# Two-layer graph-and-sequence kernel: set-up loads in another order, single buffers in other memory, offsets of four instruction streams

## The chip, the cores and the metric

The kernel runs on one core of one Trainium2 chip. A core has four compute engines: TensorE (PE, with its weight loads shown as PEld), VectorE (DVE), ScalarE (ACT) and GpSimd (POOL); SyncE (SP) issues most of the DMAs here. Each engine executes its own instructions in order and waits on semaphores for the others. The metric is the device time of one execution in microseconds (us), the median of several runs.

## The reference, cut to what matters

Input x is 32 batch elements of 512 nodes with 256 features; adj is a 512 x 512 matrix of 0 and 1 for each element. Two layers, each a graph attention and a sequence block, both on a layer norm of x and added to it:

```python
x = x + L0_gnn(layernorm(x), adj, ...)   # 4 heads, masked softmax over neighbours, norm per head
x = x + L0_ffn(layernorm(x), ...)        # Mamba-2 block: W_in, conv of 4, chunked scan, norm, W_out, W_lin
x = x + L1_gnn(layernorm(x), adj, ...)   # 1 head, masked softmax, elu
x = x + L1_ffn(layernorm(x), ...)        # LSTM over the 512 steps, all 32 elements at once,
                                         # argmax gate, prefix and suffix sums
```

The first three lines are independent for each batch element. The last one walks through the 512 steps for all elements together, so it starts only when every element is through the first three.

## The kernel before, in words

`layers_per_batch` does the first three lines, `recurrence` the last. A second copy of `layers_per_batch` for general adjacency values stands behind a branch and is not executed with these inputs.

`layers_per_batch` begins with a set-up. `load_k` (line 96) and `load_row` (line 101) load the weights on SP's queue, one DMA each; `load_row` sends one row of HBM to all 128 partitions. Weights that only the set-up needs (w0t, asrc, adst, normw, woutt, wlin, w1t, a1) lie in the pool `wset`. From them PE and DVE make derived weights: the score weights sw0 (from `pwa`, lines 154 and 205) and sw1 (from `pwb`, lines 166 and 212), and wc, the product of W_out and W_lin (`pwc`, lines 243 and 247). Then `setup.close()` gives the memory of `wset` back, and the pools `io`, `one` and `two` are opened over it.

The work on an element is cut into generators that yield after each small step: `plain0` (graph attention of layer 0, lines 470 to 580), `after0` (its norm per head, lines 315 to 338), `mamba_in` and `mamba_dt` (layer norm, transposes and the time-step column of the Mamba block), `mamba` (the block itself), and `plain1` (graph attention of layer 1). `plain0` begins with two loads, adj (line 474) and x (line 476); then come the layer norm (lines 65 to 71), `x+beta` on POOL (line 479), the mask `msk` and the check `sqa` from adj, transposes into xT, `exponents` (pra, mall, mxa, rowsa, linea, pca), the transposed mask adjT from `pm`, the projection `phn` with its copies hn and hb, and the weighted sums (rb, w, pav, psu, psut, pavT). `mamba` ends with ssc, its reciprocal root (`rstd_of`, tiles ve and rs on POOL, lines 54 and 56) and the update of x (line 848).

Four streams of such parts are merged: each part has a start and an end in units of one element's period, relative to `mamba` of the same element (0 to 1), and the step with the smallest due time is emitted next. `PACE` places the steps within `mamba`.

```python
    streams = [
        each((0.0, 1.0, mamba, 0)),
        each((-0.097, -0.026, mamba_in, 0), (-0.026, 0.192, mamba_dt, 0)),
        each((0.571, 0.86, second, -1), (0.86, 1.54, first, 2)),
        each((1.65, 1.76, after0, 2)),
    ]
```

A fifth stream is `recurrence_weights` (lines 1030 to 1108): it scales and reorders the LSTM's weights on POOL and writes them to an HBM buffer `wr`, through small tiles with one buffer each. Its due times start at 3.25. The framework's scheduler then reorders what was emitted on each engine by its own estimate of when operands are ready, so an instruction with no operand from the elements can come far ahead of its due time; in the trace these weights are prepared between 18 and 142 us.

All loads and stores of elements go through SP's queue: adj, x, the spread rows rb and bc, ce, and the store X of each element after layer 1 (line 862). One buffer holds adj, four hold x.

## Time and profile before

| what | us |
|---|---|
| median of 3 runs | 4829.85 |
| lowest and highest | 4828.24, 4832.57 |
| the profiled execution's own time | 4838.21 |
| its span, first to last instruction | 4836.4 |
| busy: PE, PEld | 4191.4, 2651.5 |
| busy: DVE, ACT, POOL | 3279.3, 3068.7, 1308.8 |
| adj of elements 0, 1, 2, 3 issued at | 30.0, 37.6, 80.3, 178.4 |
| first zs of mamba, elements 0, 1, 2 | 130.7, 230.2, 330.6 |
| X stored, elements 0, 29, 30, 31 (issue) | 317.9, 3249.9, 3324.5, 3369.3 |
| mean granted TensorE clock | 0.965 |

Busy is the time in which an engine executes an instruction. The page cuts the span into 40 slices of 121 us and shows busy tenths for each. The timeline lists instructions with start, duration, and in brackets the idle time of the engine just before them and what ended it. "SPq" and "ACTq" are DMA issues by those engines' sequencers. A load is asked for at its issue and can be used some microseconds later; the trace shows both ends, the issue by SPq and the first instruction that had waited for it. Durations below come from the profiled execution, which took 8.4 us more than the median.

### The profile page before, as it was taken

The numbers are of one execution on the slowest core, as the hardware profiler recorded it, in microseconds if no ns is written. First come the engines' busy times: TensorE is split into PE (matmuls) and PEld (weight loads), VectorE is DVE, ScalarE is ACT, GpSimd is POOL, SyncE is SP. The second block draws the span as 40 slices with busy tenths as digits, with TensorE's granted clock in tenths as the row PEclk, the third lists the DMA queues.
The fourth block names the chain that finished last, engine by engine and source line by source line (L and its number), as shares of the span: only waits on it lengthen the run. The fifth ranks groups of instructions, "written<-read, shape, count | busy, mean of one in ns | idle before, by whom it ended". The sixth has DMA issues, their size and how long they took to land. (4 is left out here: it accounts for less than half of the span.)

```text
span 4836.4 us, 126769 instructions
## 1 busy us (share of the span) xinstructions
PE 4191.4 (87%) x52926; PEld 2651.5 (55%) x52926; DVE 3279.3 (68%) x8670; ACT 3068.7 (63%) x6724; POOL 1308.8 (27%) x1012
## 2 busy tenths in 40 slices
PE   4888888888888888888888888886999999999993
PEld 2444444444554444544445444544777777777772
DVE  3567666676666666666666666664677777777776
ACT  2677667776677767677677776764555555555552
POOL 4333343333433334333343333431000000000000
PEclk7899999999999999999999999998999999999997
DMA  3221122211222112221112211111111111111115
GB/s 109 64 67 61 55 70 66 65 62 55 67 65 69 57 60 62 71 69 57 60 59 73 69 57 60 53 44 60 37 39 42 38 43 41 41 40 39 42 39 159
DMA packets 273746, 288.34 MB, mean 60 GB/s; under 512 B 152844, under 2 KB 224488, under 8 KB 270984
## 3 DMA queue, kind: packets, MB, share of 16 engines
q1 hardware_dynamic: 269784, 270.26, 19.0%
q10 hardware_dynamic: 3216, 9.81, 0.7%
q8 instruction: 418, 6.85, 0.6%
q14 instruction: 168, 1.38, 0.1%
q0 software_dynamic: 160, 0.04, 0.0%
HBM read 226.04 MB, written 37.11 MB: 54 GB/s over the span
## 5 line engine op out<-in xcount | busy, mean ns | idle before, releaser
L1260 PEld LDWEIGHTS pg<-wall,h 128*32 128x32 f32 x24528 | 476.7, 109 | 228.5 <-DVE h L1335 226.8
L1260 PE MATMUL pg<-wall,h 128*32 128x64 f32 x24528 | 561.2, 239 | 34.6 <-DVE h L1335 10.6
L1236 PE MATMUL pu<-xTr,wall 128*128 128x256 f32 x2048 | 565.5, 399 | 0.0
L467 DVE SCALAR_TENSOR_TENSOR w<-w,adjT 128x1024 f32<-128x1024 f32 x256 | 348.2, 1381 | 247.4 <-ACT w L461 247.4
L1320 ACT ACTIVATE z<-pg 128x64 f32<-128x64 f32 (+1 forms) x1536 | 345.8, 241 | 129.9 <-PE pg L1260 90.2
L1237 ACT ACTIVATE xu<-pu,wall 128x256 f32<-128x256 f32 x512 | 243.2, 475 | 278.6 <-PE pu L1236 278.6
L743 ACT ACTIVATE g<-bc,cs 128x128 f32<-128x128 f32 x1024 | 322.0, 391 | 139.7 <-PE py L811 139.7
L693 DVE SCALAR_TENSOR_TENSOR acc<-px,convw,acc 128x511 f32<-128x511 f32 (+2 forms) x480 | 347.3, 746 | 76.6 <-ACT acc L688 68.7
L461 ACT ACTIVATE w<-rb,neg,colsa 128x512 f32<-128x512 f32 x512 | 387.5, 806 | 10.2 <-DMA rb<-linea 5.8
L1236 PEld LDWEIGHTS pu<-xTr,wall 128*128 128x128 f32 x2048 | 348.8, 190 | 63.7
L533 PE MATMUL pav<-w,hb 128*64 128x512 f32 x1024 | 352.6, 615 | 21.9 <-DVE w L467 21.9
L830 PE MATMUL po<-wc,xh 128*128 128x256 f32 x1024 | 282.8, 422 | 96.8 <-POOL xh L800 96.8
L729 POOL TENSOR_TENSOR ce<-ce,cT 128x384 f32<-128x384 f32 x128 | 185.1, 1475 | 667.2 <-ACT cT L701 650.3
L54 POOL TENSOR_SCALAR ve<-mv 128x4 f32<-128x4 f32 x32 | 6.2, 193 | 1317.5 <-DVE mv L1161 1317.5
L1250 PE MATMUL pg<-turner,xu 128*32 128x64 f32 (+2 forms) x12288 | 324.3, 238 | 0.4 <-issue 0.3
L945 PE MATMUL pov<-wb,wv 128*128 128x257 f32 x1024 | 246.2, 393 | 90.4 <-DVE wv L467 90.4
L672 PE MATMUL px<-mT,win 128*128 128x512 f32 x640 | 306.9, 610 | 0.0
L830 PEld LDWEIGHTS po<-wc,xh 128*128 128x128 f32 x1024 | 203.1, 212 | 141.4 <-POOL xh L800 111.1
L1330 ACT ACTIVATE tc<-z 128x64 f32<-128x64 f32 x512 | 131.6, 257 | 224.1 <-DVE z L1328 224.1
L945 PEld LDWEIGHTS pov<-wb,wv 128*128 128x128 f32 x1024 | 193.6, 194 | 135.3 <-DVE wv L467 105.6
L1250 PEld LDWEIGHTS pg<-turner,xu 128*32 128x32 f32 x12288 | 265.6, 110 | 3.0 <-issue 1.8
L56 POOL TENSOR_TENSOR rs<-ve,mhalf 128x4 f32<-128x4 f32 (+1 forms) x192 | 256.0, 1334 | 15.9
(245 smaller groups left out, 8615.4 us busy)
## 6 DMA issues: line engine op xcount, KB each, us to landing
bc<-line SPq DMA_DIRECT2D x128, 512.0 KB
adj<-in_adj_dram SPq DMA_DIRECT2D x32, 1024.0 KB
rb<-linea SPq DMA_DIRECT2D x64, 512.0 KB
ce<-line SPq DMA_DIRECT2D x64, 384.0 KB
x<-in_x_dram SPq DMA_DIRECT2D x32, 512.0 KB
X<-x SPq DMA_DIRECT2D x32, 512.0 KB
xt<-X SPq DMA_DIRECT2D x128, 128.0 KB
x<-X SPq DMA_DIRECT2D x128, 128.0 KB
```

What stands on the lines that cost most here:

```text
L461: nc.scalar.activation(w[:, t, k, :], rb[:, k, :], AF.Relu, bias=neg1, scale=cols[:, 2 * m + t, h + k : h + k + 1],)
L467: nc.vector.scalar_tensor_tensor(w[:, :, k, :], w[:, :, k, :], 1.0, edges, ALU.add, ALU.mult)
L533: nc.tensor.matmul(pa[k * HO : (k + 1) * HO, :], hb[:, j, 2 * q + k, :], w[:, t, k, :], start=(j == 0), stop=(j == NT - 1),)
L672: nc.tensor.matmul(pz, win[:, k, col : col + P], mT[:, k, :], start=(k == 0), stop=(k == DK - 1))
L693: nc.vector.scalar_tensor_tensor(acc[:, s:], pz[:, : N - s], convw[:, cc, k : k + 1], acc[:, s:], ALU.mult, ALU.add)
L743: nc.scalar.activation(g[:, i, k, :], bc[:, k, i * P : (i + 1) * P], AF.Relu, bias=cs[:, i, 2 * cc + k : 2 * cc + k + 1], scale=-1.0,)
L830: nc.tensor.matmul(po[:, i * D : (i + 1) * D], xh[:, cc, it * P : (it + 1) * P], wc[:, cc, :], start=(cc == 0), stop=(cc == NC - 1),)
L945: nc.tensor.matmul(po[:, : D + 1], ws[j // 2][:, j % 2, 0, it * P : (it + 1) * P], wb[:, j, :], start=(j == 0), stop=(j == NT - 1),)
L1236: nc.tensor.matmul(pu, wih[:, k, u, :], xT[:, k, :], start=(k == 0), stop=(k == DK - 1))
L1250: nc.tensor.matmul(p[q * GB : (q + 1) * GB, :], xu[:, 2 * q + half, r : r + GB], turner[:, s:e], start=True, stop=(t == 0),)
L1260: nc.tensor.matmul(p[q * GB : (q + 1) * GB, :], h[:, k, :], whh[:, k, q, s:e], start=(start and k == 0), stop=(k == DK - 1),)
L1320: nc.scalar.activation(z[:, J + s0 : J + e0], p[:, : e0 - s0], AF.Tanh)
```

## The change

It has four parts. The loads of the set-up get another order on the same queue: first x of element 0, then w0t, asrc, adst, w0, adj of element 0, then beta and the other rows, then the Mamba weights, and last those for layer 1 and wc. For this the pool `io` is opened before the set-up, so that x and adj of element 0 have memory of their own, and `plain0` uses them for b = 0.

Five tiles of the Mamba part with one buffer each (csr, ce, bT, cT, ssr) move from the pool `one` to a new pool `mam`, opened where `wset` was closed, so they take the set-up's memory.

Each tile of `recurrence_weights` is now begun by a POOL copy of one column of the x of the element that is current in the merge (`begun`, `now`). So the tile's loads cannot start before that x is there.

Some offsets of the streams and of `PACE` change in the second or third digit.

```diff
+    io = ctx.enter_context(tc.tile_pool(name="io", bufs=2))
+    def load_x(b):
+        x = io.tile([P, NT, D], F32, tag="x", bufs=4, name=f"x{b}")
+        nc.sync.dma_start(out=x, in_=a.x[b].rearrange("(i p) d -> p i d", p=P))
+        return x
+    def load_adj(b):
+        adj = io.tile([P, NT, N], I32, tag="adj", bufs=1, name=f"adj{b}")
+        nc.sync.dma_start(out=adj, in_=a.adj[b].rearrange("(i p) j -> p i j", p=P))
+        return adj
+    x0 = load_x(0)
...
-    w0 = load_k(a.w0, D, "w0")
     w0t = load_k(a.w0t, D, "w0t", wset)
     asrc = load_k(a.asrc, T0, "asrc", wset)
     adst = load_k(a.adst, T0, "adst", wset)
+    w0 = load_k(a.w0, D, "w0")
+    adj0 = load_adj(0)
+    beta = load_row(a.beta, "beta")
     bias0 = load_row(a.bias0, "bias0")
     gamma = load_row(a.gamma, "gamma")
-    beta = load_row(a.beta, "beta")
+    alog = load_row(a.alog, "alog")
+    blin = load_row(a.blin, "blin")
     win = load_k(a.win, DIN, "win")
     convw = load_k(a.convw, 4, "convw")
     convb = load_k(a.convb, 1, "convb")
     dtb = wp.tile([NH, 1], F32, name="dtb")
     nc.sync.dma_start(out=dtb, in_=a.dtb.rearrange("o h -> h o"))
-    alog = load_row(a.alog, "alog")
     dcol = load_k(a.dcol, 1, "dcol")
+    w1t = load_k(a.w1t, D, "w1t", wset)
+    a1 = load_k(a.a1, 2, "a1", wset)
+    w1 = load_k(a.w1, D, "w1")
     normw = load_k(a.normw, 1, "normw", wset)
     woutt = load_k(a.woutt, DI, "woutt", wset)
     wlin = load_k(a.wlin, D, "wlin", wset)
-    blin = load_row(a.blin, "blin")
-    w1 = load_k(a.w1, D, "w1")
-    w1t = load_k(a.w1t, D, "w1t", wset)
-    a1 = load_k(a.a1, 2, "a1", wset)
...
     setup.close()
-    io = ctx.enter_context(tc.tile_pool(name="io", bufs=2))
+    mam = ctx.enter_context(tc.tile_pool(name="mam", bufs=1))
...
+        x, adj = (load_x(b), load_adj(b)) if b else (x0, adj0)
...
-        csr = one.tile([P, N], F32, tag="csr", name=f"csr{b}")
+        csr = mam.tile([P, N], F32, tag="csr", name=f"csr{b}")
...
-    PACE = ((0, 0.0), (10, 0.4), (17, 0.693), (STEPS[mamba], 1.0))
+    PACE = ((0, 0.0), (10, 0.41), (17, 0.7), (STEPS[mamba], 1.0))
...
-        each((-0.097, -0.026, mamba_in, 0), (-0.026, 0.192, mamba_dt, 0)),
-        each((0.571, 0.86, second, -1), (0.86, 1.54, first, 2)),
-        each((1.65, 1.76, after0, 2)),
+        each((-0.117, -0.026, mamba_in, 0), (-0.004, 0.184, mamba_dt, 0)),
+        each((0.571, 0.86, second, -1), (0.86, 1.52, first, 2)),
+        each((1.65, 1.75, after0, 2)),
...
+        now = lambda: states[int(min(at))]["x"][:, 0, 0:1]
-        streams.append(3.25 + (nb - 8) / 64 * n for n, _ in enumerate(recurrence_weights(nc, rw, a, wr)))
+        streams.append(3.25 + (nb - 8) / 64 * n for n, _ in enumerate(recurrence_weights(nc, rw, a, wr, now)))
...
+    def begun(t, *columns):
+        for n in columns or (0,):
+            nc.gpsimd.tensor_copy(t[:, n : n + 1], now())
+        return t
...
-                raw = tile_(P, 4 * J, f"rwraw{q % 2}")
+                raw = begun(tile_(P, 4 * J, f"rwraw{q % 2}"))
```

The same goes for ce, bT, cT and ssr as for csr, and for the tiles rwl, rbl, the two small rwraw and the rwt of fw and bw as for the last line.

More of the change, by code (lines that the diff above doesn't have):

```diff
@@ L340, in attention0 @@
     def attention0(b, state):
-        adj = io.tile([P, NT, N], I32, tag="adj", bufs=1, name=f"adj{b}")
-        nc.sync.dma_start(out=adj, in_=a.adj[b].rearrange("(i p) j -> p i j", p=P))
-        x = io.tile([P, NT, D], F32, tag="x", bufs=4, name=f"x{b}")
-        nc.sync.dma_start(out=x, in_=a.x[b].rearrange("(i p) d -> p i d", p=P))
+        x, adj = (load_x(b), load_adj(b)) if b else (x0, adj0)
         xn = two.tile([P, NT, D], F32, tag="rowa", name=f"xn{b}")
@@ L470, in plain0 @@
     def plain0(b, state):
-        adj = io.tile([P, NT, N], I32, tag="adj", bufs=1, name=f"adj{b}")
-        nc.sync.dma_start(out=adj, in_=a.adj[b].rearrange("(i p) j -> p i j", p=P))
-        x = io.tile([P, NT, D], F32, tag="x", bufs=4, name=f"x{b}")
-        nc.sync.dma_start(out=x, in_=a.x[b].rearrange("(i p) d -> p i d", p=P))
+        x, adj = (load_x(b), load_adj(b)) if b else (x0, adj0)
         xn = two.tile([P, NT, D], F32, tag="rowa", name=f"xn{b}")
@@ L654, in mamba_dt @@
         yield
-        ce = one.tile([P, NC, N - P], F32, tag="ce", name=f"ce{b}")
+        ce = mam.tile([P, NC, N - P], F32, tag="ce", name=f"ce{b}")
         for k in range(2):
@@ L682, in mamba @@
         xh = two.tile([P, NC, N], F32, tag="wide", bufs=4 if odd is not None else 3, name=f"xh{b}")
-        bT = one.tile([DS, N], F32, tag="bT", name=f"bT{b}")
-        cT = one.tile([P, N], F32, tag="cT", name=f"cT{b}")
+        bT = mam.tile([DS, N], F32, tag="bT", name=f"bT{b}")
+        cT = mam.tile([P, N], F32, tag="cT", name=f"cT{b}")
         def convolved(cc):
@@ L837, in mamba @@
             nc.tensor.matmul(pss[32 * cc : 32 * (cc + 1), :], ones[:, :32], zs[:, cc, :], start=True, stop=True)
-        ssr = one.tile([P, N], F32, tag="ssr", name=f"ssr{b}")
+        ssr = mam.tile([P, N], F32, tag="ssr", name=f"ssr{b}")
         nc.scalar.copy(ssr, pss)
@@ L1027, in layers_per_batch, with recurrence_weights @@
         nc.vector.tensor_scalar(odd, pf[:1, :1], P - 0.5, None, ALU.is_lt)
-def recurrence_weights(nc, pool, a, wr):
+def recurrence_weights(nc, pool, a, wr, now):
     Q, J = 4, 64
@@ L1052, in ordered @@
         return t
-    wl = tile_(P, 2 * DK, "rwl")
+    def begun(t, *columns):
+        for n in columns or (0,):
+            nc.gpsimd.tensor_copy(t[:, n : n + 1], now())
+        return t
+    yield
+    wl = begun(tile_(P, 2 * DK, "rwl"), 0, DK)
     for q in range(Q):
@@ L1063, in recurrence_weights @@
     nc.gpsimd.tensor_tensor(wl[:, :DK], wl[:, DK:], wl[:, :DK], ALU.subtract)
-    bl = tile_(P, 2, "rbl")
+    bl = begun(tile_(P, 2, "rbl"))
     nc.sync.dma_start(out=bl, in_=a.bl.to_broadcast([P, 2]))
-    b = [tile_(P, 4 * J, f"rwraw{n}") for n in range(2)]
+    b = [begun(tile_(P, 4 * J, f"rwraw{n}")) for n in range(2)]
     for t, src in zip(b, (a.bih, a.bhh)):
@@ L1079, in recurrence_weights @@
     for n, src in enumerate((a.fw, a.bw)):
-        t = tile_(P, W, "rwt")
+        t = begun(tile_(P, W, "rwt"))
         for q in range(Q):
```

## The prediction

> **What bounds the kernel now.** I read the page's slices first, then the sums by stage, then the timeline of the first 140 us and of one element in the middle (1355 to 1456 us).

> ```profile
> span 4836.4 us, 126769 instructions
> PE   4888888888888888888888888886999999999993
> PEclk7899999999999999999999999998999999999997
> ```

> ```profile
> 400.00:3000.00 2600.00, 2248.00 (x11012) 1243.53 (x11012) 1744.47 (x3421) 1856.63 (x3232) 993.24 (x669) 0.98 0.20 64
> 3400.00:4836.00 1436.00, 1334.39 (x38980) 1064.89 (x38968) 1079.00 (x4317) 743.70 (x2667) 40.97 (x67) 0.98 0.19 49
> ```

> The columns of the second fence are stretch, length, busy PE, PEld, DVE, ACT, POOL, clock, DMA share, GB/s. There are three stages: a start-up of some 130 us (first slice: PE 4 tenths), 32 elements at a steady pace, and the recurrence from about 3380 us on, which the change does not touch. The stores of elements 0 and 29 are issued at 317.9 and 3249.9 us: 2932.0 / 29 = 101.1 us an element. In that stage PE is busy 86%, ACT 71%, DVE 67%, so no engine is full: PE's waits follow chains through the other engines. A gain can thus come from the start-up, once, or from the pace, 32 times.

> The start-up (start, length, engine, line, instruction, idle before):

> ```profile
> 22.19 1.84 PE L166 MATMUL pwb<-a,w1t 128*128 128x2 f32 x8 [13.06 <-DMA a<-in_a_dram]
> 29.96 0.38 SPq L474 DMA_DIRECT2D adj<-in_adj_dram  x1
> 35.43 2.00 ACT L483 ACTIVATE sqa<-adj,neghalf 128x2048 bf16<-128x2048 int32 x1 [19.55 <-DMA adj<-in_adj_dram]
> 40.26 2.08 ACT L71 ACTIVATE xn<-x,off,rs 128x256 f32<-128x256 f32 x4 [2.74 <-DVE off L69]
> 48.01 0.15 DVE L431 TENSOR_TENSOR mxa<-mall,sgn 12x1 f32<-12x1 f32 x1
> 51.18 5.51 PE L507 MATMUL phn<-w,xT 128*128 128x256 f32 x16
> 90.52 1.22 DVE L333 TENSOR_REDUCE vs<-sq 128x16 f32<-128x1024 f32 x1 [1.18 <-ACT sq L331]
> 94.96 0.10 POOL L1049 MEMSET rwt<- 128x2 f32 x1 [1.89 <-DMA wr<-rwt]
> 96.46 0.21 POOL L54 TENSOR_SCALAR ve<-vs 128x16 f32<-128x16 f32 x1
> 124.02 0.87 SPq L448 DMA_DIRECT2D rb<-linea  x2
> 128.60 0.81 ACT L461 ACTIVATE w<-rb,neg,colsa 128x512 f32<-128x512 f32 x1 [5.21 <-DMA rb<-linea]
> ```

> The first element's adj and x are asked for only at 30 us, when the set-up's memory is free, so ACT stands idle for 19.55 us. Then the preparation of the recurrence's weights (lines 1049 to 1106) runs from 18 to 142 us on POOL and SP, between the first element's steps: `vs` is ready at 91.74, yet its `ve` comes at 96.46, behind weight tiles that wait for their own stores.

> **The change, part by part.**

> *The first element (gain).* The order of the built program's instructions has x0 first on SP, then w0t, asrc, adst, w0, adj0, the rows beta, bias0, gamma, alog, blin, then win. Landing times by the rates of this trace: 1 MB of adj takes 5.47 us from issue to use (29.96 to 35.43), of which 3.1 us are transfer at the 333 GB/s of the best slice, so 2.3 us are lead. x0, w0t, w0 and adj0 are 2.1 MB: 0.79 + 2.3 + 6.3 = 9.4 us for adj0, and about 5 us for x0. The next rows are slow: in the slice of 5 to 10 us, which holds bias0, gamma and beta sent to 128 partitions each, only 69 GB/s move.

> ```profile
> GB/s 125 69 232 207 84 28 241 333 291 7 174 55 7 52 52 54 234 82 84 73 0 0 55 57 79 248 80 46 119 214 62 3 6 99 0 113 202 0 2 0
> ```

> On ACT `xn0` stands behind `sqa0` (adj0) and `aneg` (alog): alog lands about 5 us after adj0, so xn0 starts at 14.2 instead of 40.26. `pra0` ends 7.0 us later, as before, at 21.2. Behind it PE now has pwb, which waits for a1. In before a1 comes at 22.19 with 3.43 MB ahead of it; now 3.94 MB are ahead, 1.5 us more, while normw (issue 2.01 us) is no longer ahead of it: 22.0. pwb takes 1.84 us, its copies on DVE stand ahead of mxa0: 24.6 instead of 48.01, 23.4 us earlier. After `pm`, PE has one matmul of phn0, then all of pwc (5.53 us), then the rest of phn0. wlin lands at about 26, before PE is there (28), but the 5.53 us, which in before lay ahead of the element's start, now lie in its path: 23.4 - 5.5 = 17.9 us earlier from there on.

> Costs 0 and why: the copies of the single mamba buffers to the set-up's memory add a wait on the set-up's last reader, but csr0, the first, is written at 120.87 in before, wc ends near 34 now. x1, adj1 and rb0 queue behind the weights on SP; by the same rates rb0's first half lands near 33, its first reader (ACT w) stands behind hn0 at about 36. If the loads are 4 us later than that, the gain falls by what is over 3 us.

> *The weights leave the start-up (gain).* `ve` comes when `vs` is ready: 4.63 us (96.46 to 91.83). The tiles between gamma's product and x's sum go: 0.66. Those around the next layer norm's ve and rs: 0.87 + 0.65. rb of element 1 is issued at 124.02 because SP waits for a weight store; linea1 is issued at about 118 after the new order on ACT, 2 us more for its landing gives 120, so w1 starts 4.0 us earlier. Sum 10.8. Both parts: 28.7 us earlier at mamba's start of element 0 (130.7 in before).

> *The weights in the steady stage (loss).* Each weight tile now begins with a POOL copy of a column of the current x. The built order puts it right after x+blin, and what uses the tile soon after:

> ```profile
> 1426.00 2.91 POOL L588 TENSOR_TENSOR x<-x,blin 128x1024 f32<-128x1024 f32 x1 [1.14 <-ACT xm L71]
> 1429.77 2.44 POOL L479 TENSOR_TENSOR x<-x,beta 128x1024 f32<-128x1024 f32 x1 [0.87 <-ACT xn L71]
> 1430.02 0.37 SPq L862 DMA_DIRECT2D X<-x  x1
> 1434.50 0.19 POOL L54 TENSOR_SCALAR ve<-ssc 128x4 f32<-128x4 f32 x1 [2.28 <-DVE ssc L844]
> 1435.82 0.48 DVE L848 SCALAR_TENSOR_TENSOR x<-po,rs,x 128x256 f32<-128x256 f32 x1 [1.42 <-POOL rs L56]
> 1437.63 0.68 ACT L433 ACTIVATE rowsa<-pra,mxa 12x512 f32<-12x512 f32 x1 [0.73 <-DVE mxa L431]
> 1438.36 0.41 PE L438 MATMUL pca<-ident,rowsa 8*128 8x8 f32 x4
> ```

> For the 8 tiles of wih (elements 7 to 16, POOL): copy to 1429.15; SP's load is issued then (adj ahead of it is long gone, its 1421.90 issue); a load of this kind is used at most 1.85 us after its issue (66.28 to 68.13), so 1431.0; four scalings of 1.37 us together to 1432.4; x+beta, which now stands behind them, 2.44 to 1434.8; a memset, which waits for the store of the tile (2.1 us, hidden by x+beta) to 1435.0. So `ve<-ssc` is at 1435.1 instead of 1434.50: 0.6 us. For the 8 tiles of whh: x+beta comes before the scalings, but four loads go out with X's 512 KB store between them; the last is issued at 1430.95 and has that store ahead of it, so it lands near 1433.8, scalings to 1435.2: 0.75 us. The six small steps before (elements 2 to 6) end before the next POOL work at 1440.29: 1 us in all.
> Who waits: behind ve stand rs, the update of x on DVE, mall, rowsa and, without a gap in the trace, PE's pca. So the delay passes on nearly whole: 8 x 0.6 + 8 x 0.75 + 1 = 11.8, times 0.9, +11 us. In the same elements x's load goes out behind the tile's store; it is used at 1440.12, some 2.5 us after its landing, so that cover holds unless the weight load is 2.5 us late.

> [...]

> *The order inside an element.* The new pace and offsets move little, the same in every element I compared: px's third pair of matmuls behind pav/psu; the copy avs ahead of acc (psut, whose wait before was 1.34 us, comes 0.66 us sooner, but the o it feeds stands on DVE behind the conv steps, which are busy from 1377.4 on); praw behind the last pm (0.4 us later, but its ee stands on ACT behind adjT until 1441.2 anyway); hb's products bunched, so da comes 0.33 us later, where PE then waits 0.43 us less for w. I take 0, with 0.3 us to either side: -10 to +10 us over 32 elements.

> **Sum**: -28.7 + 11 + 0 = -18 us. The profiled execution took 4838.21 us with a span of 4836.4, 8.4 us (0.17%) over the median of 4829.85; the steps would be the same in both. So 4829.85 - 18 = 4812 us.

> **The rivals.**
> 1. *Forecast*, -10 to -26 us, 4812.
> 2. *The weight tiles cost nothing in the steady stage* (ve has slack, or the loads land sooner) and the start-up gives all: -29 us, to -36 if a1 and the rows land 7 us sooner than the slow slice says. For it: POOL is idle for 2.28 us before ve. Against: x+beta fills that. 4800.
> 3. *The gain is used up within the noise*: a1 or wlin later by 5 to 8 us (every load is on one queue[...]), or 0.3 us more an element. 4825.
> 4. *Slower*: the weight load lands late, POOL stands still in order, and ve, x's update and PE's pca wait in 16 elements. The trace has one such case: a weight store issued at 83.00, behind an adj load of 80.34, held POOL until 87.28, 4.3 us. With 4.3 us, wih gives 1429.2 + 4.3 + 1.37 + 2.44 + 0.1 = 1437.4, 2.9 us late, whh 1430.95 + 4.3 + 1.4 = 1436.7, 2.2 us: 41 us, and 4829.85 - 28.7 + 41 = 4842. It decides from 28.7 / 16 = 1.8 us a tile on. Against: the adj load is through by 1427.
> That the loads do not really come first, or that the weights stay at the start, is nearly excluded: both stand so in the built order.

> **The numbers.** Less than 0.2% (9.7 us) cannot be told from no change here. Forecast 0.56 and rival 2 0.18 are both faster by more: 0.74. Rival 3, with the forecast's weak end: 0.16. Rival 4, with a pace worse by over 0.6 us: 0.10. The range goes from 4793 (rival 2 with a pace better by 0.2 us) to 4838 (rival 4 short of its full price).

> **What would show it.** Right: adj0 used at about 9, xn0 at 14, pwb at 22, pwc ahead of phn0, mamba's first zs of element 0 near 102 instead of 130.7; no weight step on POOL before the third element; `ve<-ssc` 0.5 to 1 us later after x+blin in elements 7 to 24, and stores 101.1 us apart in the last elements, some 101.7 in those with tiles. Wrong: a start-up shorter by under 20 us, POOL waits for the weight loads above 2.5 us, or a pace off 101.1 where no tile is.

## The result, and the profile after: 15 us slower

| | before | after |
|---|---|---|
| median of 12 runs each, us | 4828.23 | 4843.56 |
| lowest and highest, us | 4824.08, 4834.49 | 4835.56, 4853.0 |
| the profiled execution's own time, us | 4838.21 | 4843.21 |
| its span, us | 4836.4 | 4840.9 |
| first zs of mamba, element 0, us | 130.7 | 102.3 |
| X stored, elements 0, 29, 31, us | 317.9, 3249.9, 3369.3 | 282.8, 3255.9, 3372.0 |
| store to store, mean of elements 0 to 29, us | 101.1 | 102.5 |

The ratio after / before is 1.0031, 95% interval 1.0022 to 1.0040. The start-up gained what was forecast (28.4 us at the first zs, 35.1 at the first store); each element then takes 1.4 us longer, and 29 of them use the gain up. (The profiled execution of before lies 10 us above its median, so the two spans differ by only 4.5 us.)

The page's slices of after, and then the sums by stage with the columns as before:

```profile
span 4840.9 us, 126700 instructions
PE   6888888888988888888888888886999999999993
PEclk8999999999999999999999999998999999999997
```

```profile
400.00:3000.00 2600.00, 2265.76 (x10862) 1241.51 (x10862) 1733.26 (x3367) 1838.90 (x3199) 1027.76 (x764) 0.97 0.21 64
3400.00:4836.00 1436.00, 1339.20 (x39099) 1069.38 (x39098) 1080.18 (x4325) 746.86 (x2678) 41.06 (x67) 0.98 0.19 49
```

In the same 2600 us PE executes 150 instructions fewer and is busy 18 us longer. Fewer matmuls that last longer: the granted clock, 0.98 before, is 0.97 here. That small digit is where the case begins.

The timeline of the start-up (start, length, engine, line, instruction, idle before):

```profile
11.42 1.28 ACT L494 ACT_TABLE_LOAD   x1 [11.42 <-DMA adj<-in_adj_dram]
14.81 2.06 ACT L71 ACTIVATE xn<-x,off,rs 128x256 f32<-128x256 f32 x4
21.67 1.87 PE L182 MATMUL pwb<-a,w1t 128*128 128x2 f32 x8
24.05 0.14 DVE L445 TENSOR_TENSOR mxa<-mall,sgn 12x1 f32<-12x1 f32 x1
28.17 4.35 PE L259 MATMUL pwc<-wlin,woutt 128*128 128x256 f32 x16
71.71 0.21 POOL L54 TENSOR_SCALAR ve<-vs 128x16 f32<-128x16 f32 x1 [6.47 <-DVE vs L350]
102.30 0.60 ACT L691 ACTIVATE zs<-pz 128x512 f32<-128x512 f32 x1
```

adj0 is used at 11.4 us (9.4 was forecast), pwb runs at 21.7, mxa at 24.1, pwc lies ahead of the rest of phn0, and `ve` waits for `vs` and no longer for weights.

Where the pace goes shows in windows of 3.41 us around the wait of `po` for xh. First after, around pst and po of element 20, then the kernel with only the loads and pools changed (f3 below) around po of its element 21. Columns: stretch, length, busy PE, PEld, DVE, ACT, POOL, granted clock, DMA share, GB/s.

```profile
2190.29:2193.70 3.41, 1.36 (x5) 0.30 (x2) 3.38 (x5) 2.94 (x4) 3.41 (x3) 1.00 0.45 154
2193.70:2197.11 3.41, 3.04 (x4) 1.12 (x4) 2.62 (x5) 0.00 (x0) 1.49 (x2) 0.50 0.00 0
...
2224.42:2227.84 3.42, 0.99 (x5) 0.89 (x6) 1.70 (x3) 3.37 (x7) 1.69 (x1) 1.00 0.70 252
2227.84:2231.25 3.41, 3.41 (x10) 2.65 (x9) 3.38 (x2) 3.41 (x6) 2.90 (x1) 0.50 0.14 55
2231.25:2234.66 3.41, 3.41 (x21) 2.81 (x19) 0.67 (x1) 0.68 (x2) 2.43 (x1) 1.00 0.44 154
...
2296.10:2299.52 3.42, 3.08 (x4) 1.12 (x4) 2.62 (x5) 0.00 (x0) 1.47 (x2) 0.50 0.00 0
```

```profile
2301.67:2305.08 3.41, 2.14 (x12) 1.50 (x10) 1.48 (x8) 2.75 (x5) 2.17 (x3) 1.00 0.03 1
2305.08:2308.49 3.41, 1.48 (x7) 1.33 (x8) 1.69 (x3) 3.41 (x7) 2.09 (x2) 1.00 0.87 293
2308.49:2311.90 3.41, 3.41 (x20) 2.95 (x19) 3.38 (x2) 3.29 (x5) 2.54 (x2) 1.00 0.05 16
```

In the traces of before and after the granted clock is 1.00 or 0.50 and changes on a fixed grid: all its changes lie a whole number of 3.4133 us apart, to within 0.01 us. A step of this grid is called a window here. Where PE was busy for 0.99 or 1.36 us of a window, the next one runs at 0.50. In f3 the same wait is split between two windows, with 2.14 and 1.48 us of work, and the clock stays at 1.00. The matmuls around these waits in the timeline of after, and po in that of f3:

```profile
2191.53 1.13 PE L794 MATMUL pst<-xdd,bn 128*128 128x512 f32 x2 [1.00 <-POOL xdd L787]
2194.07 3.48 PE L794 MATMUL pst<-xdd,bn 128*128 128x512 f32 x4 [1.41 <-POOL xdd L787]
2226.85 5.84 PE L841 MATMUL po<-wc,xh 128*128 128x256 f32 x18 [3.19 <-POOL xh L811]
```

```profile
2307.01 4.15 PE L841 MATMUL po<-wc,xh 128*128 128x256 f32 x18 [3.20 <-POOL xh L811]
```

For po the wait and the instructions are the same, and they take 1.69 us more at half clock. An element has two places where this mostly happens: behind pst (waits of 1.0 and 1.4 us for xdd), some 50 us after its first zs, and behind po (3.2 us), some 83 us after. Sorting elements by the half-clock windows in them gives, in before: none 99.16 us (one element), the first alone 100.49, the second alone mostly 100.85, both 102.2. From 200 to 3200 us before has 42 half-clock windows, after 58: 24 of elements 1 to 29 of after have both (7 in before), and last 102.4 where no tile lies in them.

Why both, always? The windows in after's elements 20 and 21 start at 2193.70, 2227.84 and 2296.10: 10 windows, and then 30 windows, 102.40 us. An element of exactly 30 windows meets the grid at the same phase as the one before it, and so has the same two half-clock windows again. In before an element with both lasts 102.2, slips by 0.2 us against the grid each time, and after at most three of them one wait straddles a border. The new order lifts it to 102.4, and it never slips. That is the theory (the *lock*, theory 1 in the expectations). That it is 102.40 and not 102.35 or 102.45 is no accident, since the length depends a little on where the grid lies in the element. In m2 (below) elements 2 to 6 last 102.43 to 102.44 us, so each meets the grid some 0.04 us later than the one before; their second window moves from 83.95 to 83.81 us after the first zs, and from 83.75 on they last 102.40 or 102.41. Element 10 (102.47) pushes it to 83.65; 11 to 14 last 102.35 to 102.39 and bring it back. So m2, whose elements reach 102.40 for some position of the grid, stays there; before, whose elements with both windows last 102.2, slips. The traces show the grid and its step of 3.413 us, not what in the chip sets it.

### The profile page after: what moved, and what is told of

The parts are those of the page before. It is cut to its first block, busy times and chain, and to the rows that moved or that the text cites. A ratio compares the mean times of both kernels' runs of the same rounds, so it can differ in the third digit from the quotient of the medians.

```text
span 4840.9 us, 126700 instructions
## 1 busy us (share of the span) xinstructions
PE 4238.7 (88%) x52926; PEld 2668.5 (55%) x52926; DVE 3283.9 (68%) x8670; ACT 3072.2 (63%) x6724; POOL 1332.9 (28%) x1035
## 3 DMA queue, kind: packets, MB, share of 16 engines
q14 instruction: 166, 1.36, 0.1%
## 5 line engine op out<-in xcount | busy, mean ns | idle before, releaser
L841 PE MATMUL po<-wc,xh 128*128 128x256 f32 x1024 | 296.8, 438 | 96.3 <-POOL xh L811 96.3
L54 POOL TENSOR_SCALAR ve<-mv 128x4 f32<-128x4 f32 x32 | 6.2, 193 | 1320.0 <-DVE mv L1179 1320.0
L841 PEld LDWEIGHTS po<-wc,xh 128*128 128x128 f32 x1024 | 213.4, 222 | 144.6 <-POOL xh L811 109.6
L56 POOL TENSOR_TENSOR rs<-ve,mhalf 128x4 f32<-128x4 f32 (+1 forms) x192 | 257.7, 1342 | 15.9
```

The lines of the kernel that those rows point to most:

```text
L841: nc.tensor.matmul(po[:, i * D : (i + 1) * D], xh[:, cc, it * P : (it + 1) * P], wc[:, cc, :], start=(cc == 0), stop=(cc == NC - 1),)
```

## The experiments

Rivals: (a) the new order costs 1.3 us an element by its dependencies; (b) the weight tiles on POOL cost it. Medians are in the tables; "ratio" is against before on the same chip. "Both" counts elements 1 to 29 with both half-clock windows.

**One part at a time.** e1 has the old offsets in the changed kernel; e2 only the new offsets in the kernel before; e3 is the changed kernel without the copies, f3 the same with the old offsets:

```diff
 def begun(t, *columns):              # e3, f3
-    for n in columns or (0,):
-        nc.gpsimd.tensor_copy(t[:, n : n + 1], now())
     return t
```

> The changed kernel with the offsets and the pace list of the kernel before: inside an element the instructions stand in the order of before, while the loads, the pools and the gated weight tiles stay new. Theory 1[...]: X3 stores 101.1 us apart as before, first silu of element 0 near 102, about 4800 us. Rival a (the new order costs 1.3 us by its dependencies): the same, about 4800. Rival b (the weight tiles on POOL cost the 1.3 us): still 102.4 us apart, about 4843.

> The kernel before with only the new offsets and pace list. Theory 1 and rival a: X3 stores 102.4 us apart, start-up unchanged, 4828 + 31 x 1.35 = about 4870 us. Rival b: 101.1 us apart, about 4828.

> The changed kernel without the one-column copies that hold each weight tile back, so that the weight tiles are loaded and folded in the start-up again; the order inside an element is that of the changed kernel. Theory 1 and rival a: 102.4 us apart still; start-up longer by the 10.8 us that the prediction gave the tiles, about 4850 us. Rival b: 101.1 us apart, about 4810.

> The changed kernel with the old offsets and without the one-column copies: the kernel before with only the loads and the pools changed, weight tiles folded at the start. Pace of before (101.1) and the start-up of the run without the copies (first store 25 us earlier than before): 4828 - 25 = about 4805 us. If the 0.9 us that the run with old offsets lost per element came from the phase of the windows alone and not from the weight tiles: about 4827 again.

| run | loads, pools | copies | offsets | us | ratio | first X | store to store | both |
|---|---|---|---|---|---|---|---|---|
| f3 | new | no | old | 4806.57 | 0.9955 (0.9939 to 0.9972) | 294.1 | 100.88 | 5 |
| e1 | new | yes | old | 4826.95 | 0.9991 (0.9981 to 1.0000) | 282.6 | 102.03 | 12 |
| e2 | old | no | new | 4868.03 | 1.0081 (1.0064 to 1.0097) | 314.1 | 102.39 | 25 |
| e3 | new | no | new | 4847.80 | 1.0039 (1.0024 to 1.0053) | 292.6 | 102.40 | 29 |

The offsets alone cost 38 us (e2 against its before, 4830.0), or 41 (e3 against f3), with no weight tile in the elements: after's pace doesn't need rival b. In e3 all elements from 2 to 28 last 102.38 to 102.43 us. Yet e1 missed its 4800: with the old offsets the copies cost 1.15 us an element (against f3). Each of the two parts costs the pace (measured from f3) 33 to 44 us alone, and both together (102.52 - 100.88) x 29 = 48 us: lock and tiles do not add up (below). So even with the old offsets the change would have gained next to nothing (e1, 0.9991).

**Half of the offsets.** n1 has of the new offsets only those of mamba_in and mamba_dt, n2 only that of layer 0's attention; base f3.

> The kernel with only the loads and pools changed, and of the new offsets only those of mamba_in and mamba_dt: of one element's rows 4 move on TensorE, 18 on VectorE. Theory 1: an element with both half-clock windows lasts 102.2 us plus what the moves cost; up to 0.1 us nothing is locked and the time is 4807 to 4815; near 0.2 it locks at 102.40 exactly and the time is 4845. Rival a: a part of the 41 us in proportion, 4807 to 4848, without elements of exactly 102.40.

> The kernel with only the loads and pools changed, and of the new offsets only that of layer 0's attention (0.86 to 1.52): 12 rows move on TensorE, 11 on ScalarE, 19 on VectorE. Theory 1: all or nothing, 4807 to 4815 unlocked or 4845 with elements of exactly 102.40. Rival a: the rest of the 41 us that the run with only the offsets of mamba_in and mamba_dt leaves.

n1: 4831.34 us (ratio 0.9996, 0.9987 to 1.0004), n2: 4849.37 (1.0034, 1.0022 to 1.0045). n2 is locked, 26 elements at 102.38 to 102.42. n1 answers neither "all or nothing" nor a share of a dependency: its elements with both windows last 102.26 to 102.36 in the main, slip by 0.1 us, and so come three to seven in a row where f3 has one to three: 19 elements of 29 instead of 5, and 25 us. The price of 0.1 us is in how long the phase lingers.

**Shorten the element.** The last product of xh and zs on VectorE; j1 with the old offsets, j2 with the new, both without copies:

```diff
-            nc.gpsimd.tensor_tensor(y, y, zs[:, cc, :], ALU.mult)
+            (nc.vector if cc == NC - 1 else nc.gpsimd).tensor_tensor(y, y, zs[:, cc, :], ALU.mult)
```

> The kernel with only the loads and pools changed (old offsets, no one-column copies), and the last of the four xh x zs products of each element on VectorE (0.6 us) in place of POOL (1.7 us): the wait of po for xh falls from 3.2 to about 2.0 us. Path alone: 31 x 1.2 = 37 us less than 4807, 4770. If the shorter wait also brings no half-clock window behind po any more: another 31 x 0.8, 4745.

> The same edit of the product on the kernel with the loads, pools and new offsets changed (no one-column copies), which took 4848 us with the product on POOL. Theory 1 (the new order costs some 0.2 us per element by itself and 1.1 us by the lock on 102.4 us): at 1.2 us less per element the lock is out of reach, so it loses its extra cost too: within 10 us of the same edit under the old offsets, about 4750 to 4780. Rival a (1.3 us by dependencies): 4848 - 37 = 4811, still 40 us above the same edit under the old offsets.

j1: 4786.95 us (0.9899, 0.9862 to 0.9937), j2: 4790.44 (0.9910, 0.9893 to 0.9926). The new offsets, which cost 41 us with the product on POOL, cost 3.5 us with it on VectorE by the medians, and (100.28 - 99.92) x 29 = 10 us by the profiled paces. The four runs of j1 lie between 4763.52 and 4799.53, so the cost may be anything up to some 25 us, but rival a would have kept the 40. An element with both windows lasts 101.0 us in j1 and 101.33 in j2, out of reach of 102.4. Elements without a half-clock window last 98.86 and 99.23: 0.37 us is what the new order costs by itself. Both runs missed their forecasts of 4745 to 4780: f3's element without such a window lasts 99.16, so of the 1.2 us taken from the wait only 0.3 lay on the path.

**Lengthen it, and move nothing.** All runs so far change an order as well. The next four only add useless matmuls behind psc, the matmuls whose sums ssc reads (m2: 2 columns, 0.25 us; m3: 256 columns; m4: two of these, 0.38 us each; m5: as m3 on e3); the order of the other instructions in the elements stays the same on every engine.

```diff
+        for m in range(1):           # m4: range(2)
+            nc.tensor.matmul(pst[:, NT : NT + 256], ssr[:, :P], ssr[:, :256], start=True, stop=True)
```

> The kernel with only the loads and pools changed (4807 us), with one useless matmul behind the four psc in each element (moving operand of 2 columns, about 0.26 us on TensorE's own sequence). All other instructions keep their order on every engine. Lock: an element with both half-clock windows goes from 102.2 to about 102.45 us, at or above 30 windows, so the phase no longer slips and the mean is 102.4: 4807 + 31 x 1.4 = about 4848 us. Proportional: 31 x 0.26 = 8 us, 4815.

> The same with 256 columns, about 0.43 us per element. Lock: the mean stays at 102.4, because elements with one window fewer are shorter than 102.4 and those with both are longer, and the phase settles between: 4848 us again. Proportional: 4820.

> Two such matmuls of 256 columns, about 0.86 us per element. Lock: 102.4 still, 4848 us. Proportional: 4834.

> The kernel with loads, pools and new offsets changed (no one-column copies, 4848 us), with one useless matmul of 256 columns behind psc. Lock: it costs nothing, the mean stays at 102.4 and the time at 4848 us. Proportional: 4861.

| run | added to | us | ratio | store to store | half-clock windows, 200 to 3200 us |
|---|---|---|---|---|---|
| f3 | | 4806.57 | 0.9955 (0.9939 to 0.9972) | 100.88 | 37 |
| m2 | f3 | 4851.69 | 1.0049 (1.0032 to 1.0066) | 102.40 | 57 |
| m3 | f3 | 4854.95 | 1.0058 (1.0041 to 1.0075) | 102.41 | 56 |
| m4 | f3 | 4825.04 | 0.9990 (0.9980 to 1.0000) | 101.43 | 29 |
| m5 | e3 | 4847.16 | 1.0039 (1.0025 to 1.0053) | 102.15 | 51 |

The first 0.25 us costs 45 us, nearly 6 times what it adds to 31 elements. Some 0.4 us costs 3 us more, nothing in the new order (m5). 0.76 us is *27 us cheaper than 0.25*: there only one half-clock window is left in most elements (101.81 us), which I had not expected. Without such a window an element of m4 lasts 100.13 us, 0.97 more than in f3; over 31 elements that is 30 us, yet m4 is only 18 us slower than f3, with 29 half-clock windows for 37. No sum of dependencies with fixed durations falls when work is added. The totals of m3 and m5 came as forecast, the way there did not: m3's elements last 99.69 to 105.25 us with a mean of 102.41, and m5's alternate between 103.06 and 101.74 us. And m5's elements without a half-clock window last 100.04 us, m3's 99.69: again 0.35 us for the new order by itself. The sums by stage of f3, m2 and m4:

```profile
400.00:3000.00 2600.00, 2242.94 (x11063) 1238.75 (x11063) 1759.61 (x3437) 1865.82 (x3257) 992.23 (x668) 0.98 0.20 63
```

```profile
400.00:3000.00 2600.00, 2249.90 (x10947) 1246.32 (x10945) 1722.20 (x3385) 1834.85 (x3196) 975.42 (x660) 0.97 0.21 63
```

```profile
400.00:3000.00 2600.00, 2259.55 (x11085) 1253.26 (x11084) 1742.97 (x3412) 1856.55 (x3236) 984.12 (x665) 0.98 0.21 64
```

In 2600 us m2 gets through fewer instructions on every engine than m4, at 0.97 of the clock against 0.98.

**What missed.** e4 copies ssc once more on POOL; f1 and f2 fill waits of PE with useless matmuls; f4 issues the twelve po matmuls of xh 0 to 2 ahead of the four of xh 3.

```diff
+            ss2 = small.tile([P, NT], F32, tag="ss2", name=f"ss2_{b}_{m}")   # e4
+            nc.gpsimd.tensor_copy(ss2, ssc)
...
+                    if it == 0 and cc == 2:                                  # f1, f2
+                        for m in range(5):
+                            nc.tensor.matmul(po[:, D:], xh[:, cc, :P], wc[:, cc, :], start=False, stop=False)
```

> The changed kernel with one more instruction in each element: POOL copies the 128x4 tile ssc once on the way from the sum of squares to the update of x (about 0.27 us on the path). TensorE and ScalarE keep the order of the changed kernel. Theory 1: an element is no longer 30 windows long, the lock slips, elements without one of the two half-clock windows come back, and the mean falls to 101 to 102 us in spite of the longer path: 4800 to 4840. Rival a: 31 x 0.27 = 8 us more, about 4852.

> The changed kernel with five useless matmuls (128x256, same operands as the one before them, into columns that the next group overwrites) on TensorE in each element, placed where po waits 3.2 us for the last xh from POOL. No other engine's order moves apart from three small POOL instructions. Theory 1 (half-clock windows cost the time): the window at 83.8 us after the first silu goes, the 102.4 us lock slips, an element has one window or fewer, pace 100 to 101, about 4780 to 4800 us, faster although work was only added. Rival a (dependencies of the new order): no gain, 4843, or up to 31 x 5 x 0.42 = 65 us more if the matmuls don't fit in the wait.

> The changed kernel with useless matmuls in four waits of TensorE per element: before pst (3 of 128x512), before the pcv transposes (2 of 36x512), inside pov (4 of 128x255) and inside po (5 of 128x256), some 6.5 us of TensorE work per element that computes nothing; the scheduler also moves some 40 rows. Theory 1: half-clock windows between 200 and 3200 us fall from 56 to under 10, pace 98 to 100, about 4730 to 4770 us. Rival a: no gain or slower, 4843 to 5000.

> The changed kernel with the po matmuls in another order: the twelve that need xh 0 to 2 first, then the four that need xh 3, so that useful work fills the wait of 3.2 us. Nothing else moves. If only the wait counts: 31 x 3.2 = 99 us less, 4744. Theory 1: the half-clock window behind it goes as well, 1.4 to 1.7 us per element more, and the lock is broken: 4690 to 4710. If po is not on the path that sets the pace: 4843 or the 4790 of the filled wait.

e4 took 4850.81 us, f1 4908.01, f2 4932.91, f4 4845.69. e4 hit rival a's number (4852), but it left most elements with one window and still at 102.4: some rows move on VectorE, so it is no clean test of either. In f1 the window behind po went, as wanted, but the scheduler put five more of the po matmuls behind the pxT transposes, where PE waits 0.9 us and then has them on its path. f2 moved whole groups in the same way. In f4 PE's wait of 3.2 us became one of 2.65 us at pxT, with its own half-clock window. So these runs don't test a filled wait cleanly; the four above move nothing.

**Two last ones**, on j1: j3 with the second xdd product on VectorE as well, j4 with the copies.

> The kernel with the loads and pools changed and the last xh x zs product on VectorE (4787 us), with also the second of the three xdd products on VectorE, so that pst no longer waits for three POOL products in a row; some 24 rows move on TensorE and 30 on VectorE. If pst is on the path: 1.0 to 1.4 us less per element, and fewer windows behind pst: 4730 to 4755 us. If VectorE's queue only passes the wait on: 4787.

> The kernel with all parts of the change but the offsets, and the last xh x zs product on VectorE. Against the same without the one-column copies (4787 us): start-up 10 us shorter, weight tiles between the elements cost the 14 us that were counted under the old offsets: 4780 to 4800 us.

j3 took 4794.87 us (0.9922, 0.9901 to 0.9944), no better than j1: 25 of elements 1 to 29 have two half-clock windows, at 55 and 79 us; its forecast (4730 to 4755) missed. j4 took 4811.57 (0.9965, 0.9948 to 0.9981), 25 us over j1 and above its forecast: first X store at 283.4 instead of 294.6, but 101.45 us an element instead of 99.92. j1 and j2, which can't be told apart by their runs, are the best kernels of the study, 1.0 and 0.9% below before.

## Why the prediction was wrong, point by point

**The start-up: right in sum.** Forecast 28.7 us earlier at zs of element 0, measured 28.4 (102.3). Of the steps, xn0 came at 14.81 (14.2 forecast), pwb at 21.67 (22.0), mxa at 24.05 (24.6). The split was less good, and that the sum fits so well is luck: at this zs the loads give 25.2 us (f3, 105.5), where 17.9 were forecast, the copies 6.2 (e1, 99.3), where 10.8 were, and the new offsets take 3.0 back. Of the loads' surplus 1.2 us is pwc, which took 4.35 us in place of 5.53; where the rest comes from was not followed up.

**"The order inside an element. ... I take 0 ... -10 to +10 us": this step failed.** The new order costs 41 us (e3 against f3). What the prediction looked at, the moves themselves, was nearly right: they cost 0.35 us an element (j2 against j1, m5 against m3, elements without a half-clock window), just outside the band of 0.3, or 11 us in 31 elements. What it put at nothing, without a reason, is the other 30 us: the period decides which elements get half-clock windows, and 102.40 us gives both windows to all of them. The granted clock of 0.98 stood in the windows that the prediction quotes, and was read as a constant.

**"The weights in the steady stage": mis-sized, then hidden.** Forecast 11 us. In kernels that don't stay at 102.4 the copies cost (102.03 - 100.88) x 29 = 33 us (e1) and (101.45 - 99.92) x 29 = 44 us (j4 against j1). In after they cost (102.52 - 102.40) x 29 = 3.5 us against e3. The time by which the tiles hold `ve` back behind ssc, summed over the elements, is 16 us in e1, 35 in j4 and 6 in after; what e1 loses beyond it goes with more elements that have both half-clock windows (12 for 5). POOL and SP in the timeline of after, element 14:

```profile
1613.59 2.90 POOL L599 TENSOR_TENSOR x<-x,blin 128x1024 f32<-128x1024 f32 x1 [1.14 <-ACT xm L71]
1616.55 1.06 POOL L1068 COPY rwraw<-x 128x1 f32<-128x1 f32 x1
1617.64 0.33 SPq L1112 DMA_DIRECT2D rwraw<-in_wih_dram  x1
1620.32 1.36 POOL L1063 TENSOR_SCALAR rwt<-rwraw 128x64 f32<-128x64 f32 x4 [2.71 <-DMA rwraw<-in_wih_dram]
1621.64 2.35 POOL L490 TENSOR_TENSOR x<-x,beta 128x1024 f32<-128x1024 f32 x1
1624.43 0.19 POOL L54 TENSOR_SCALAR ve<-ssc 128x4 f32<-128x4 f32 x1
```

Three terms of it were off. The one-column copy lasts 1.06 us, where the forecast had it done 0.24 us after x+blin. The load is used 2.68 us after its issue, not 1.85. And the element read for the slack, from 1355 to 1456 us, lies mostly in element 12 of before, the longest of elements 1 to 29, 103.42 us with four half-clock windows: ssc was ready 95.0 us after its first zs, in the others 90.8 to 93.8. A `ve` that a tile holds until 94.1 to 94.6 is no loss there, but one of 2.0 to 2.2 us in an element without the second window (e1, elements 10, 12 and 13, ssc at 92.1). The lock hides it for the same reason: in after ssc mostly comes at 94.0, and most tiles delay `ve` by 0.7 us or less (elements 8 and 12: 2.0 and 2.1 us). Rival 4, with 41 us for late loads and 4842 us in all, has the measured total by luck: POOL's longest wait for such a load in after is 2.8 us, not 4.3, and the tiles' 6 us are not what made after slow.

**The sum.** Forecast -28.7 + 11 + 0. Measured in the profiled executions: -35.1 at the first store, +41.1 from there to the store of element 29 (2973.1 against 2932.0 us), -3.3 in the last two elements, +1.8 in the recurrence. "A pace off 101.1 where no tile is" was named as what would make it wrong, and is what happened: elements 25 to 28 of after have no tile and last 102.4 us. So was a wait of POOL for the weight loads above 2.5 us (8 waits for wih, 21.3 us in all).

## What to carry to other kernels

In a loop whose TensorE waits come to 2 to 3 us (here 3.2 us at po, 2.4 in all at pst), sort the iterations by the granted clock before reading one of them: the "typical" iteration may be the one with most half-clock windows. Compare the period with multiples of the step on which the granted clock changes in the trace (3.413 us here): with a period at 30 of them the time was a staircase, where a matmul of 0.25 us in each element cost 45 us and two of 0.38 us cost 18. Judge a small reordering only beside the same kernel lengthened by a useless instruction that moves nothing, and take the waits away (here one product moved to VectorE) rather than tune offsets on the stairs.
